# A cross-attention kernel with 8192 keys: the first slots in smaller pieces, the rows of maxima and sums beside V, the last unit's output in one PSUM bank

## The chip, the cores and the metric

The kernel runs on one core of a Trainium2 chip. The core has five engines that this text names: TensorE (PE in the profile; its weight loads are PEld), VectorE (DVE), ScalarE (ACT), GpSimd (POOL) and the queue engine SP, which issues most of the DMAs. Each engine works through its own instructions in order, and engines wait for one another by semaphores. TensorE writes only to PSUM, a small memory of eight banks of 2 KB per partition; everything else lies in SBUF. The metric is device time in microseconds (us) of the whole launch, the median of several runs.

## What is computed

A small transformer layer stack on 2 x 512 latent tokens of 512 features: cross-attention to 2 x 8192 context tokens, then windowed self-attention, then a mixture of experts. Only the first stage is touched. It is

```python
q = layernorm(x) @ Wq.T + bq            # 2 x 512 x 512
k, v = ctx @ Wk.T + bk, ctx @ Wv.T + bv # 2 x 8192 x 512
att = einsum('bhqd,bhkd->bhqk', q, k) / sqrt(32)   # 16 heads
att = where(mask == 0, -inf, att)
out = einsum('bhqk,bhkd->bhqd', softmax(att), v)
x = x + out @ Wo.T + bo
```

All inputs are float32. The mask of these inputs is all ones, but the kernel handles any.

## The kernel before

The heads are worked off four at a time, since four heads of 32 features fill the 128 rows of TensorE. A batch with one such group of heads is a *unit*; there are 8. The keys come in chunks of 512, so a unit has 16 chunks, and there are 128 chunks in all. The softmax is exact and takes two passes over the keys of a unit: the first finds the row maxima, the second computes the exponentials with the maximum taken off, their sums and the weighted values. A unit's keys are projected ahead of the first pass and kept for the second; one load of a context chunk serves the keys of one unit and the values of the unit before it, where both are of one batch.

The main loop (line 399) runs over 128 + 18 *slots*. In slot n the kernel loads context for slot n + 1, projects the keys of chunk n (`project_k`, two halves of 256 keys), finds the maxima of chunk n - 1 (`max_part`, four times, once for each 128 queries), projects the values of chunk n - 16 (`project_v`, two halves), and does scores, exponentials and values of chunk n - 18 (`scores` and `values`, four times). `LAG` is that 18. The body of a slot has four *quarters*, i = 0 to 3, each with one `max_part`, one `scores` and one `values`; keys go with quarters 0 and 1, values with quarters 2 and 3.

So the slots fall into three kinds. In the first slots (1 to 17) there are only keys and maxima. From slot 18 to 127 all of it runs. From slot 128 there are no more keys and maxima.

The steps that matter here:

- *First slots.* `max_part` has its own branch for them. TensorE writes the scores of two heads into a pair buffer of two banks (L276, tile sx), and takes the mask off with four bf16 matmuls from a row of it (L282, operand mk, loaded from mrow_h by L221); VectorE reduces each pair (L287, into mst). There are three pair buffers (`a_pairs`), and the pool for everything else has two banks (`a_ps1`). The queries (L173, 4 matmuls of the whole 128 x 128 array with 512 columns, L177 copies them out) are made one group of heads at a time: the first ahead of the loop, the others out of the list `later`, one entry at the end of each slot. The list also holds the layernorm and the four transposes (L98) of the second batch.
- *Keys and values.* Both use TensorE in column tiles: a matmul with 32 weight columns fills a quarter of the array, and four run side by side (L239 for keys, tile pk; L255 for values, tile pv). ScalarE copies keys out (L243), VectorE values with their bias (L260, tile vt).
- *Maxima from slot 18 on.* Scores in one bank for each head (L295), and one VectorE operation with the mask, which also takes the maximum (L300).
- *End of the first pass of a unit* (`max_finish`, at the end of the slot after its last chunk, so at slots 16, 32, ...): VectorE reduces mst (L309), splits the float32 maximum into three bf16 parts (L311, L313, tile mrep), TensorE turns them into rows (L316, tile pm), ScalarE copies them to SBUF (L321, tile mT). `scores` takes them off with bf16 matmuls (L337).
- *Second pass.* TensorE scores (L331, tile sc), ScalarE the exponential (L344, tile pt; acc for the first of a unit), TensorE the values (L353, tile av), VectorE adds them to the unit's output (L361, tile avs). GpSimd adds the exponentials into acc (L365); near the end of the loop VectorE does that.
- *End of a unit* (`finish`, in the slot of the next unit's second chunk, so at slots 35, 51, ...): TensorE sums acc over the keys (L373, tile sm), ScalarE copies (L377, tile rl), VectorE takes reciprocals (L379), GpSimd multiplies (L381).

The order on each engine is the order of the program, except that a scheduler at build time moves an instruction ahead of ones that can't start yet. A pool of PSUM banks gives a bank out again as soon as its last reader is done, and TensorE waits for that. From slot 18 on one pool has all 8 banks, and a quarter takes 9 or 10 of them in turn.

Ahead of the loop SP loads in this order: x of the first batch, wq, wk, the first context chunk, x of the second batch, wv. The first mask load follows the second context chunk. The mask rows in DRAM (mrow, mrow_h) are written by `mask_rows` after the first query.

After the loop eight output projections (L106, tile po) follow; the last unit's `finish` stands after the second of them.

## Time and profile before

| | |
|---|---|
| median of 3 runs | 3814.18 us (3814.16 to 3819.29) |
| the profiled execution's own time | 3813.35 us |
| its span, first to last instruction | 3811.6 us |
| first slots, 24.0 to 254.2 us of the span | 230.2 us |
| slots 18 to 127, to 2438.8 | 2184.6 us |
| last slots, to the first output projection at 2666.1 | 227.3 us |
| the rest of the program | 1145.5 us |
| mean granted TensorE clock | 0.995 |
| bytes moved | 438.07 MB, mean 115 GB/s |

A row of the timeline has the start, the duration of a merged group, engine, line, operation, output and inputs, shapes, how many instructions, and in brackets how long the engine had stood idle and for whom. Durations of merged groups overlap on TensorE, so the cost of a block is the distance to the start of the next one. "DVE 60%" is a mean over stages of different kinds: by the windows, VectorE is busy 163.75 of the first slots' 230.20 us and 208.90 of the last slots' 227.30.

### The profile page before, as it was taken

To read this page: it belongs to the slowest core of one execution; us is meant where nothing else is said; L and a number is where in the kernel's file an instruction comes from. 1 tells how busy PE (TensorE), PEld (TensorE's weight loads), DVE (VectorE), ACT (ScalarE), POOL (GpSimd) and SP (SyncE) were. 2 spreads that over 40 slices of the span, in tenths; PEclk is the share of its full clock that TensorE was granted. 3 is DMA by queue.
4 is the path that set the end of the run, shared out by engine and by line. 5 is a ranking of instruction groups with operands and counts; after the bars stand their busy time and mean duration, and the time that the engine had idled before them with its cause. 6 is when DMAs were issued, how large, how long until landed. Compare 5 with 4: busy or idle time off the path is not lost.

```text
span 3811.6 us, 99469 instructions
## 1 busy us (share of the span) xinstructions
PE 3741.4 (98%) x43060; PEld 1835.4 (48%) x43060; DVE 2293.9 (60%) x5420; ACT 1601.8 (42%) x2965; POOL 2069.0 (54%) x523
## 2 busy tenths in 40 slices
PE   8999999999999999999999999999999999999998
PEld 3345554554554555555455455444454444444444
DVE  5777777777777777777777777799853600000000
ACT  1125555555555555555555555677463001111110
POOL 0029998998998998899899899600200000000000
PEclk9999999999999999999999999999999999999999
DMA  5222211222213333222222122222201178888885
GB/s 189 89 73 71 71 62 66 71 71 71 69 63 111 122 120 104 61 68 71 71 71 71 57 71 71 71 79 71 80 25 43 61 240 287 288 286 287 287 284 172
DMA packets 143735, 438.07 MB, mean 115 GB/s; under 512 B 9408, under 2 KB 11728, under 8 KB 117856
## 3 DMA queue, kind: packets, MB, share of 16 engines
q1 hardware_dynamic: 137856, 419.33, 33.0%
q0 software_dynamic: 5200, 12.30, 1.3%
q8 instruction: 337, 5.52, 0.6%
q14 instruction: 102, 0.84, 0.1%
q10 hardware_dynamic: 240, 0.08, 0.0%
HBM read 423.21 MB, written 8.47 MB: 113 GB/s over the span
## 4 chain that ended last, share of the span: by engine, by line
PE 87%; DVE 2%; ACT 2%; issue 1%; DMA 0%; POOLq 0%; DVEq 0%; ACTq 0%
PE av L353 13%; PE sx L295 12%; PE sc L331 12%; PE pv L255 11%; PE pf L857 11%; PE pk L239 10%; PE py L875 5%; PE pf L810 3%; PE sc L337 3%; PE po L106 2%; PE pqkv L535 2%; PE pso L833 1%; PE tp L98 1%; DVE junk L300 1%; ACT sb L611 1%
## 5 line engine op out<-in xcount | busy, mean ns | idle before, releaser
L365 POOL TENSOR_TENSOR acc<-acc,pt 128x2048 f32<-128x2048 f32 x437 | 1991.9, 4558 | 445.6 <-ACT pt L344 444.9
L344 ACT ACTIVATE pt<-sc,mbias 128x512 f32<-128x512 f32 x2016 | 1220.1, 690 | 951.2 <-PE sc L337 949.7
L300 DVE CUSTOM_DVE_ANT_0 junk<-sx,mk 128x512 bf16<-128x512 f32 x1776 | 1228.1, 691 | 550.0 <-PE sx L295 352.7
L331 PE MATMUL sc<-qT,kt 32*128 32x512 f32 x4096 | 546.4, 594 | 0.0
L353 PE MATMUL av<-pt,vt 128*32 128x512 f32 x4032 | 540.6, 605 | 2.8 <-DVE mst L300 2.8
L255 PEld LDWEIGHTS pv<-wv_sb,ctx_t 128*32 128x32 f32 x16384 | 457.6, 110 | 155.0 <-DVE mst L300 101.4
L295 PE MATMUL sx<-kt,qT 32*128 32x512 f32 x3552 | 509.1, 640 | 0.9 <-DVE vt L260 0.9
L239 PE MATMUL pk<-ctx_t,wk_sb 128*32 128x256 f32 x8192 | 497.5, 384 | 2.1 <-DVE mst L300 2.1
L255 PE MATMUL pv<-wv_sb,ctx_t 128*32 128x128 f32 x16384 | 495.1, 273 | 1.3 <-DVE avs L361 1.3
L857 PE MATMUL pf<-wt,xinT 128*128 128x512 f32 x1024 | 459.4, 593 | 1.1
L239 PEld LDWEIGHTS pk<-ctx_t,wk_sb 128*32 128x32 f32 x8192 | 263.3, 111 | 295.7 <-DVE mst L300 104.7
L361 DVE TENSOR_TENSOR avs<-av,avs 128x512 f32<-128x512 f32 x504 | 345.4, 685 | 2.7 <-PE av L353 2.5
L331 PEld LDWEIGHTS sc<-qT,kt 32*128 32x128 f32 x4096 | 245.6, 184 | 201.0 <-issue 160.3
L864 DVE TENSOR_TENSOR eo<-pf,sg 128x512 f32<-128x512 f32 x64 | 44.3, 692 | 459.0 <-PE pf L857 459.0
L857 PEld LDWEIGHTS pf<-wt,xinT 128*128 128x128 f32 x1024 | 193.0, 190 | 221.0 <-issue 213.2
L786 POOL DMA_INDIRECT xin<-h_dram,idx x16 | 15.9, 992 | 435.1 <-PE tp L98 310.0
L881 POOL DMA_INDIRECT out_x<-y,idx x16 | 25.3, 1579 | 408.9 <-DVE y L880 408.9
L353 PEld LDWEIGHTS av<-pt,vt 128*32 128x32 f32 x4032 | 81.7, 108 | 325.9 <-DVE mst L300 281.0
L875 PE MATMUL py<-wt,eoT 128*128 128x512 f32 x512 | 222.3, 592 | 0.0
L862 ACT ACTIVATE sg<-pf 128x512 f32<-128x512 f32 x64 | 38.2, 597 | 426.9 <-PE pf L857 426.9
L337 PE MATMUL sc<-mT,neg 32*128 32x512 bf16 x2048 | 207.8, 374 | 0.0
L295 PEld LDWEIGHTS sx<-kt,qT 32*128 32x128 f32 x3552 | 139.9, 182 | 138.2 <-DVE mst L300 92.3
(159 smaller groups left out, 2471.1 us busy)
## 6 DMA issues: line engine op xcount, KB each, us to landing
ctx_t<-in_ctxT SPq DMA_DIRECT2D x160, 1024.0 KB, 6.0
wt<-in_gw SPq DMA_DIRECT2D x64, 1024.0 KB, 4.9
wt<-in_up SPq DMA_DIRECT2D x64, 1024.0 KB, 4.9
wt<-in_down SPq DMA_DIRECT2D x64, 1024.0 KB, 6.3
mk<-mrow SPq DMA_DIRECT2D x111, 256.0 KB, 3.5
ctx<-in_wqkv SPq DMA_DIRECT2D x3, 1024.0 KB, 5.1
mk<-mrow_h SPq DMA_DIRECT2D x17, 128.0 KB, 2.9
x_sb<-in_x SPq DMA_DIRECT2D x2, 1024.0 KB, 10.7
```

What stands on the lines that cost most here:

```text
L239: nc.tensor.matmul(pk[ts(h, DK), :], lhsT=wk_sb[:, c, ds(g * P + h * DK, DK)], rhs=ctx_t[slot, b][:, c, hs], start=(c == 0), stop=(c == DC ...
L255: nc.tensor.matmul(pv[ts(k, DK), i, :], lhsT=ctx_t[slot, b][:, c, ds((2 * half + i) * P + k * DK, DK)], rhs=wv_sb[:, c, ts(g, P)], start=( ...
L295: nc.tensor.matmul(sm, lhsT=qT[r, g, ds(b * S + c * P, P)], rhs=k_t[s][r, :], start=True, stop=True)
L300: nc.vector.tensor_tensor_reduce(out=junk, in0=ss[h], in1=mk_t[s], scale=1.0, scalar=-3.0e38, op0=ALU.add, op1=ALU.max, accum_out=mst[u][: ...
L331: nc.tensor.matmul(sc, lhsT=k_t[s][r, ts(ch, P)], rhs=qT[r, g, ts(b, S)], start=True, stop=False)
L337: nc.tensor.matmul(ss[h], lhsT=neg[r, :], rhs=m_t[u][r, :], start=False, stop=True)
L344: nc.scalar.activation(pt[:, h, :], ss[h], AF.Exp, bias=mbias[:, b, cc : cc + 1], scale=SCALE)
L353: nc.tensor.matmul(av[ts(h, DK), :], lhsT=v_t[s][:, ch, ts(h, DK)], rhs=pt_t[s, ch][:, h, :], start=True, stop=True,)
L361: nc.vector.tensor_tensor(avs[u], av, avs[u], ALU.add)
L365: eng.tensor_tensor(acc[u], acc[u], pt_t[s, ch], ALU.add)
L857: nc.tensor.matmul(pf, lhsT=xinT[:, c, :], rhs=wt[:, c, :], start=False, stop=(c == DC - 1))
L875: nc.tensor.matmul(py, lhsT=eoT[:, fq * 4 + c, :], rhs=wt[:, c, :], start=False, stop=(fq == FQ - 1 and c == 3),)
```

## The change

- In slots 0 to 15 keys are projected in quarters of 128 keys, one in each quarter of a slot, one slot's first quarter at the end of the slot before. The queries use column tiles too and are cut into eight pieces of 4 matmuls (half of the queries, a quarter of the features); `later` gives out one piece in every quarter. The general pool `a_ps1` has one bank, and a second one, `a_psq`, has one for queries and transposes.
- Loads: wk and the first context chunk come ahead of wq, the mask rows and the first mask load ahead of the query.
- `max_finish` moves one slot later and keeps its reduction on VectorE; the split into three parts goes to GpSimd, from SBUF. The matmuls that make rows of it, in column tiles, go into the free half of the bank that `project_v` uses, by `beside`, two halves; ScalarE copies them from there.
- The sums of a unit go the same way, beside V in the slot of the next unit's second chunk; the reciprocals and the product follow in the slot after.
- From slot 128 `project_v` makes one block of 128 keys in each quarter. From slot 130 one bank is set aside, and the last unit's values accumulate in it by TensorE; VectorE does no additions for that unit, and its product is made on VectorE.

```diff
-        ps = first_ps.enter_context(tc.tile_pool(name="a_ps1", bufs=2, space=PSUM))
+        ps = first_ps.enter_context(tc.tile_pool(name="a_ps1", bufs=1, space=PSUM))
+        ps_q = first_ps.enter_context(tc.tile_pool(name="a_psq", bufs=1, space=PSUM))
...
         def query_in(b, c):
             xn = tmp.tile([P, D], F32, tag="row", name="xn")
             normalized(xn, b * (NT // B) + c, *ln[b])
-            transposed(xnT[b][:, :, ts(c, P)], xn, ps)
-        def query(b, g):
-            pq = ps.tile([P, S], F32, tag="ps", name="pq")
-            for c in range(DC):
+            transposed(xnT[b][:, :, ts(c, P)], xn, ps_q)
+        pq = {}
+        def query(b, g, half, c):
+            if c == 0:
+                pq[0] = ps_q.tile([P, S // 2], F32, tag="ps", name="pq")
+            for h in range(4):
                 nc.tensor.matmul(
-                    pq, lhsT=wq_sb[:, c, ts(g, P)], rhs=xnT[b][:, c, :],
-                    start=(c == 0), stop=(c == DC - 1),
-                )
-            nc.scalar.activation(qT[:, g, ts(b, S)], pq, AF.Identity, bias=bq_c[:, g : g + 1])
+                    pq[0][ts(h, DK), :], lhsT=wq_sb[:, c, ds(g * P + h * DK, DK)],
+                    rhs=xnT[b][:, c, ts(half, S // 2)], start=(c == 0), stop=(c == DC - 1),
+                )
+            if c == DC - 1:
+                nc.scalar.activation(
+                    qT[:, g, ds(b * S + half * (S // 2), S // 2)], pq[0], AF.Identity,
+                    bias=bq_c[:, g : g + 1],
+                )
...
-                tp = ps.tile([P, P], F32, tag="ps", name="tpk")
+                tp = (ps, ps_q)[b].tile([P, P], F32, tag="ps", name="tpk")
...
-        def project_k(slot, half):
+        def project_k(slot, part, parts=2):
             u, j = chunks[slot]
             b, g = units[u]
-            if half == 0:
+            if part == 0:
                 k_t[slot] = kp.tile([P, KC], F32, tag="k", name="kt")
-            hs = ts(half, KC // 2)
-            pk = ps.tile([P, KC // 2], F32, tag="ps", name="pk")
+            hs = ts(part, KC // parts)
+            pk = ps.tile([P, KC // parts], F32, tag="ps", name="pk")
             for c in range(DC):
                 for h in range(4):
                     nc.tensor.matmul(
...
                     )
             nc.scalar.activation(k_t[slot][:, hs], pk, AF.Identity, bias=bk_c[:, g : g + 1])
-        def project_v(slot, half):
+        def project_v(slot, lo, n):
             s = slot - NKC
-            if half == 0:
+            if lo == 0:
                 v_t[s] = vp.tile([P, KC // P, P], F32, tag="v", name="vt")
-            pv = ps.tile([P, 2, P], F32, tag="ps", name="pv")
-            for i in range(2):
+            pv = ps.tile([P, 4, P], F32, tag="ps", name="pv")
+            for i in range(n):
                 for c in range(DC):
                     for k in range(4):
                         nc.tensor.matmul(
                             pv[ts(k, DK), i, :],
-                            lhsT=ctx_t[slot, b][:, c, ds((2 * half + i) * P + k * DK, DK)],
+                            lhsT=ctx_t[slot, b][:, c, ds((lo + i) * P + k * DK, DK)],
                             rhs=wv_sb[:, c, ts(g, P)], start=(c == 0), stop=(c == DC - 1),
                         )
+            if lo >= 2 or n == 2:
+                beside(slot, lo // 2 if n == 2 else lo - 2, pv[:, 2:4].rearrange("p n k -> p (n k)"))
             nc.vector.tensor_tensor(
-                v_t[s][:, ts(half, 2), :], pv,
-                bv_b[:, ts(g, P)].unsqueeze(1).to_broadcast([P, 2, P]), ALU.add,
+                v_t[s][:, ds(lo, n), :], pv[:, 0:n, :],
+                bv_b[:, ts(g, P)].unsqueeze(1).to_broadcast([P, n, P]), ALU.add,
             )
...
                 )
-        def max_finish(u):
-            rest = ps.tile([P, 4, 4], F32, tag="ps", name="mcol")
-            nc.vector.tensor_reduce(rest, mst[u], AX.X, ALU.max)
-            for i in range(3):
-                nc.vector.tensor_copy(mrep[:, :, :, i], rest)
+        def max_finish(u, step):
+            if step == 0:
+                rest[u] = tmp.tile([P, 4, 4], F32, name="mcol")
+                nc.vector.tensor_reduce(rest[u], mst[u], AX.X, ALU.max)
+            for i in ((0,), (1, 2))[step]:
+                nc.gpsimd.tensor_copy(mrep[:, :, :, i], rest[u])
                 if i < 2:
-                    nc.vector.tensor_tensor(rest, rest, mrep[:, :, :, i], ALU.subtract)
-            pm = ps.tile([P, S], F32, tag="ps", name="pm")
-            for c in range(4):
-                nc.tensor.matmul(
-                    pm[:, ts(c, P)], lhsT=mrep[:, c, :, :].rearrange("p h r -> p (h r)"),
-                    rhs=ident_h, start=True, stop=True,
-                )
-            m_t[u] = mp.tile([P, S], BF16, tag="mT", name="mT")
-            nc.scalar.copy(m_t[u], pm)
+                    nc.gpsimd.tensor_tensor(rest[u], rest[u], mrep[:, :, :, i], ALU.subtract)
+        def beside(slot, half, dst):
+            hs = ts(half, S // 2)
+            u = units_at(slot - 2, NKC - 1)
+            if u is not None:
+                if half == 0:
+                    m_t[u] = mp.tile([P, S], BF16, tag="mT", name="mT")
+                for c in range(2):
+                    for h in range(4):
+                        nc.tensor.matmul(
+                            dst[ts(h, DK), ts(c, P)], lhsT=mrep[:, 2 * half + c, h, :],
+                            rhs=ident_h, start=True, stop=True,
+                        )
+                nc.scalar.copy(m_t[u][:, hs], dst)
+            u = units_at(slot - LAG - NKC, 1)
+            if u is not None:
+                if half == 0:
+                    rl[u] = tmp.tile([P, S], F32, tag="row", name="rl")
+                for h in range(4):
+                    nc.tensor.matmul(
+                        dst[ts(h, DK), :], lhsT=ones32, rhs=acc[u][:, h, hs],
+                        start=True, stop=True,
+                    )
+                nc.scalar.copy(rl[u][:, hs], dst)
+        def units_at(s, j):
+            return s // NKC if 0 <= s < NS and s % NKC == j else None
...
         def values(s, ch):
             u, j = chunks[s]
             first = j == 0 and ch == 0
-            av = ps.tile([P, S], F32, tag="ps", name="av")
+            last = u == len(units) - 1
+            av = avs[u] if last else ps.tile([P, S], F32, tag="ps", name="av")
             for h in range(4):
                 nc.tensor.matmul(
                     av[ts(h, DK), :], lhsT=v_t[s][:, ch, ts(h, DK)], rhs=pt_t[s, ch][:, h, :],
-                    start=True, stop=True,
-                )
-            if first:
+                    start=first or not last, stop=not last or (j == NKC - 1 and ch == 3),
+                )
+            if last:
+                pass
+            elif first:
                 avs[u] = mp.tile([P, S], F32, tag="avs", name="avs")
                 nc.vector.tensor_copy(avs[u], av)
             else:
...
                 eng = nc.gpsimd if s + LAG <= NS else nc.vector
                 eng.tensor_tensor(acc[u], acc[u], pt_t[s, ch], ALU.add)
-        def finish(u, step):
+        def finish(u, i):
             b, g = units[u]
-            if step == 0:
-                sm = ps.tile([P, S], F32, tag="ps", name="sm")
-                for h in range(4):
-                    nc.tensor.matmul(
-                        sm[ts(h, DK), :], lhsT=ones32, rhs=acc[u][:, h, :], start=True, stop=True
-                    )
-                rl[u] = tmp.tile([P, S], F32, tag="row", name="rl")
-                nc.scalar.copy(rl[u], sm)
-            for i in {0: (), 1: (0, 1), 2: (2, 3), 3: ()}[step]:
-                nc.vector.reciprocal(rl[u][:, ts(i, P)], rl[u][:, ts(i, P)])
-            if step == 3:
-                nc.gpsimd.tensor_tensor(qT[:, g, ts(b, S)], avs[u], rl[u], ALU.mult)
+            nc.vector.reciprocal(rl[u][:, ts(i, P)], rl[u][:, ts(i, P)])
+            if i == 3:
+                eng = nc.vector if u == len(units) - 1 else nc.gpsimd
+                eng.tensor_tensor(qT[:, g, ts(b, S)], avs[u], rl[u], ALU.mult)
+        def finish_last():
+            u = len(units) - 1
+            sm = ps.tile([P, S], F32, tag="ps", name="sm")
+            for h in range(4):
+                nc.tensor.matmul(
+                    sm[ts(h, DK), :], lhsT=ones32, rhs=acc[u][:, h, :], start=True, stop=True
+                )
+            rl[u] = tmp.tile([P, S], F32, tag="row", name="rl")
+            nc.scalar.copy(rl[u], sm)
+            for i in range(4):
+                finish(u, i)
         load(0)
+        wq_sb = load_w(wq, pp, "p")
         load_x(1)
         wv_sb = load_w(wv, cp, "wv_sb")
+        mask_rows()
+        load_mask(0)
         query_norm(0)
         for c in range(NT // B):
             query_in(0, c)
-        query(0, 0)
-        mask_rows()
-        load_mask(0)
-        later = [lambda g=g: query(0, g) for g in range(1, G)]
+        for i in range(4):
+            project_k(0, i, 4)
+        halves = [(half, c) for half in range(2) for c in range(DC)]
+        for half, c in halves:
+            query(0, 0, half, c)
+        later = [lambda g=g, p=p: query(0, g, *p) for g in range(1, G) for p in halves]
         later += [lambda: query_norm(1)]
         later += [lambda c=c: query_in(1, c) for c in range(NT // B)]
-        later += [lambda g=g: query(1, g) for g in range(G)]
+        later += [lambda g=g, p=p: query(1, g, *p) for g in range(G) for p in halves]
         waiting = None
         for slot in range(NS + LAG):
             if slot == LAG:
                 first_ps.close()
-                ps = es.enter_context(tc.tile_pool(name="a_ps", bufs=8, space=PSUM))
+                steady_ps = ExitStack()
+                ps = ps_q = steady_ps.enter_context(tc.tile_pool(name="a_ps", bufs=8, space=PSUM))
+            if slot == NS + LAG - NKC:
+                steady_ps.close()
+                ps = es.enter_context(tc.tile_pool(name="a_ps3", bufs=7, space=PSUM))
+                last_ps = es.enter_context(tc.tile_pool(name="a_last", bufs=1, space=PSUM))
+                avs[len(units) - 1] = last_ps.tile([P, S], F32, name="avl")
             if slot + 1 < NS + NKC:
...
-                if s >= NKC and chunks[s][1] == 1:
-                    finish(chunks[s][0] - 1, i)
-                if i < 2 and slot < NS:
+                u = units_at(s - NKC, 2)
+                if u is not None:
+                    finish(u, i)
+                if slot < NKC:
+                    if i < 3 and slot > 0:
+                        project_k(slot, i + 1, 4)
+                    elif i == 3 and slot + 1 < NKC:
+                        project_k(slot + 1, 0, 4)
+                elif i < 2 and slot < NS:
                     project_k(slot, i)
-                if i == 3 and slot > 0 and later:
+                if later:
                     later.pop(0)()
-                if i >= 2 and NKC <= slot < NS + NKC:
-                    project_v(slot, i - 2)
-            if 1 <= slot <= NS and chunks[slot - 1][1] == NKC - 1:
-                max_finish(chunks[slot - 1][0])
+                if i >= 2 and NKC <= slot < NS:
+                    project_v(slot, 2 * i - 4, 2)
+                elif NS <= slot < NS + NKC:
+                    project_v(slot, i, 1)
+                u = units_at(slot - 2, NKC - 1)
+                if u is not None and i < 2:
+                    max_finish(u, i)
             if n == 1:
-                for i in range(4):
-                    finish(len(units) - 1, i)
+                finish_last()
```

More of the change, by code (lines that the diff above doesn't have):

```diff
@@ L152, in perceiver_kernel @@
         junk = cp.tile([P, KC], BF16, name="junk")
-        wq_sb = load_w(wq, pp, "p")
         wk_sb = load_w(wk, cp, "wk_sb")
@@ L201, in perceiver_kernel @@
         ctx_t, mk_t, k_t, v_t = {}, {}, {}, {}
-        mst, m_t, acc, pt_t, avs, rl = {}, {}, {}, {}, {}, {}
+        mst, m_t, acc, pt_t, avs, rl, rest = {}, {}, {}, {}, {}, {}, {}
         def load(slot):
```

## The prediction

> **What bounds the kernel now.** I read the page first, its busy rows and its slices.
>
> ```profile
> PE 3741.4 (98%) x43060; PEld 1835.4 (48%) x43060; DVE 2293.9 (60%) x5420; ACT 1601.8 (42%) x2965; POOL 2069.0 (54%) x523
> PE   8999999999999999999999999999999999999998
> ```
>
> TensorE looks full everywhere, but a matmul's end is modelled, so a full digit can still hold waiting. What counts is the distance from one block's start to the next, and that I took from the timeline, first in the steady slots (18 to 127), where nothing waits:
>
> ```profile
> 284.09 1.14 PE L295 MATMUL sx<-kt,qT 32*128 32x512 f32 x8
> 285.06 1.04 PE L331 MATMUL sc<-qT,kt 32*128 32x512 f32 x8
> 285.91 0.39 PE L337 MATMUL sc<-mT,neg 32*128 32x512 bf16 x4
> 286.24 1.07 PE L353 MATMUL av<-pt,vt 128*32 128x512 f32 x8
> 287.12 1.93 PE L255 MATMUL pv<-wv_sb,ctx_t 128*32 128x128 f32 x64
> ```
>
> Starts differ by 0.97, 0.85, 0.33, 0.88 and, to the next sx at 288.98, 1.86. These are my TensorE prices: 4.89 us a quarter slot (4.87 with pk), 19.51 a slot; VectorE is busy 14.45 of it by the windows. 97 of the 109 slots 19 to 127 last 19.5 to 19.6 us and are TensorE's own work, which the change leaves alone. What it can win is elsewhere, in three places.
>
> First slots (1 to 17, 24.0 to 254.2 by the first sx of L276 and of L295):
>
> ```profile
> 49.72 0.40 PE L282 MATMUL sx<-mk,neg 1*128 1x512 bf16 x4
> 50.14 4.83 DVE L287 TENSOR_REDUCE mst<-sx 128x2 f32<-128x1024 f32 x4 [0.80 <-PE sx L282]
> 51.42 0.70 PE L276 MATMUL sx<-kt,qT 32*128 32x512 f32 x2 [0.46 <-DVE mst L287]
> 52.70 3.70 PE L173 MATMUL pq<-xnT,p 128*128 128x512 f32 x8
> 56.33 1.14 PE L276 MATMUL sx<-kt,qT 32*128 32x512 f32 x8
> 57.71 2.36 DVE L287 TENSOR_REDUCE mst<-sx 128x2 f32<-128x1024 f32 x2 [2.74 <-PE sx L282]
> ```
>
> Quarters 2 and 3 have no projection between them, so TensorE waits for VectorE's maxima; then the query (3.63 us) holds the maxima back and VectorE stands 2.74 us. Each waits for the other in turn: 13.88 us for a slot.
>
> Unit ends, at slots 32 + 16k and 35 + 16k:
>
> ```profile
> 547.22 0.43 DVE L309 TENSOR_REDUCE mcol<-mst 128x16 f32<-128x256 f32 x1
> 549.39 0.40 PE L316 MATMUL pm<-ident_h,mrep 128*128 128x128 bf16 x4 [1.71 <-DVE mrep L311]
> 549.72 1.14 PE L295 MATMUL sx<-kt,qT 32*128 32x512 f32 x8
> 591.87 1.04 PE L373 MATMUL sm<-acc,ones 128*32 128x512 f32 x8
> 594.07 2.58 DVE L379 RECIPROCAL rl<-rl 128x128 f32<-128x128 f32 x3 [0.23 <-ACT rl L377]
> 597.25 1.06 PE L353 MATMUL av<-pt,vt 128*32 128x512 f32 x8 [0.47 <-DVE mst L300]
> ```
>
> Slot 32 takes 21.7 us: 2.1 over, 1.71 of it TensorE waiting for VectorE's split, the rest the pm matmuls. Slot 35 takes 21.47, 1.96 over: the sums (0.86) and 1.10 of stalls behind the reciprocals, which come before the maxima that free PSUM. Six units end so inside the steady part.
>
> Last slots (128 to 145):
>
> ```profile
> 2600.73 1.14 PE L331 MATMUL sc<-qT,kt 32*128 32x512 f32 x8
> 2602.89 1.93 PE L255 MATMUL pv<-wv_sb,ctx_t 128*32 128x128 f32 x64
> 2603.81 0.68 DVE L361 TENSOR_TENSOR avs<-av,avs 128x512 f32<-128x512 f32 x1
> 2604.76 1.14 PE L331 MATMUL sc<-qT,kt 32*128 32x512 f32 x8
> ```
>
> A slot takes 12.92 here. TensorE's blocks make 4 x 2.17 + 2 x 1.86 = 12.4. VectorE has 4 x 2.28 (acc) + 4 x 0.68 (avs) + 2 x 0.42 (vt) = 12.7, in front-loaded quarters, which costs TensorE the 0.5.
>
> **The change, part by part.** *First slots.* A quarter becomes sx 0.97 + neg 0.33 + a quarter of keys + a query piece. A quarter of keys is 32 instructions of 128 columns, the form of pv: 1.86 / 2 = 0.93. A query piece is 8 instructions of 256 columns, a quarter of a pk half: 0.47. Sum 2.69. VectorE's two reductions of 1.21 make 2.42, so TensorE is the bound, and three pair buffers are just enough: a buffer is wanted again 2.7 us after its block began and is reduced by 2.6. Slots 1 to 15: 52 query quarters x 2.69 = 139.9; four with transposes (0.86) at 3.08 = 12.3; five without a piece, about 9.9 in all. That is 162. Slots 16 and 17 (1.29 x 4 + 4 x 1.86) 12.6 and, with the maxima's rows, 13.1. Together 187.7 against 230.2: minus 42.5. This includes the half clock: the granted-clock events show five stretches at 0.5 in these slots, 20.5 us long, about 10 us lost; the page's clock for the part is 0.96.
>
> Here a rule of the Trainium skill speaks against the change. "TensorEngine Tiling (Array Packing)", section Instruction Overhead, warns of about 60 cycles for each matmul and advises not to split what is already small; the query goes from 8 instructions of the whole array to 64 of 32 columns. Charged in full (an estimate, 25 ns by the 2.4 GHz in the table that opens "TensorE: Matmul & The Clock Gate"), 56 more instructions x 7 queries would be 9.8 us. The row of pk says otherwise: 32 such instructions in 1.86 us, 58 ns each for 256 columns, so a query is 3.72 against 3.63. I take the row: 0.7 us in all, already in the sum.
>
> *Start.* wk and ctx go ahead of wq; the mask rows ahead of the query. SP reaches the first mask load before the second ctx, and must wait there for mrow_h; behind it in SP's queue stands every ctx load. The mask (6.9 us to land after 3.6) allows mbias at 11 instead of 12.1, the rows are written by about 17.5, the six megabytes ahead occupy the queues until about 20.8, so ctx comes at about 24 as before. TensorE now waits for ctx (about 13.1, from the DMA bytes in order) before the transposes that began at 10.5. From there: keys 3.7, transposes 3.4, query 3.7, four pieces 1.9, a quarter of keys 0.9: 13.6, plus 1.5 for single banks (four hand-overs, 0.3 to 0.5 each by the ACT copies) and 2 for the cold clock. First maxima at about 30 instead of 24.0; the mask wait of 2.70 is then gone (counted in the 230.2). Plus 6, bounds 3 to 8.
>
> *Maxima.* The wait of 1.71 and pm's 0.33 go from slot 32 (minus 2.1). The split goes to GpSimd as five operations of 128x16. No row has that shape; between the two sizes of POOL's TENSOR_TENSOR (4558 ns at 2048, 1304 at 512) the fixed part is about 0.22 us, so 1.3 us in all, at most 6.5 if each cost as much as the 512 one. In the order of the built program they stand behind acc 58 of the unit and wait for VectorE's reduction; GpSimd, at 18.23 of 19.51, falls behind by about 3 us and gains 0.3 a quarter. Queued behind are acc's adds; they free pt, which is wanted some 12 us later, and TensorE reads mrep two quarters later: hidden. Without this cover it is the old 1.7 again. TensorE now runs 16 matmuls of 32 weight columns: pm's 83 ns each would be 1.3 us, pv's pitch of 29 ns 0.5; the form is pv's, I take 0.5 to 0.6.
>
> *Sums.* 8 matmuls (16 instructions) of 256 columns behind V: 0.93 instead of 0.86. The reciprocals are not spread as the source says: the built order has two around the end of each V half. VectorE has 3.4 us extra over three quarters with 0.4 to 0.8 free each; I leave 0.45 of the 1.10.
>
> "PSUM — Partial Sum Buffer", section PSUM bank collisions, forbids two engines in one bank and quadrant at once, even to read; here ScalarE copies the rows while VectorE wants V from the same bank. The built order makes vt wait for ScalarE's copy, so the rule shows as a wait: about 0.5 us (a copy of 256 columns is 0.3 to 0.5). Queued behind vt are the next maxima, but the trace gives VectorE 0.60 idle just there: I take nothing, 0.5 if the cover fails, two halves for 15 rows, 30 times: 15 us at worst.
>
> A unit's end: minus 2.1 + 0.55, minus 1.96 + 0.93 + 0.45, together minus 2.1; six of them minus 12.7 (bounds 5 and 17).
>
> *Last slots.* The last unit's outputs accumulate in one bank: 64 avs additions of 0.68 leave VectorE. A quarter is then TensorE 2.17 + 0.93 = 3.10, ScalarE 4 exponentials 2.42, VectorE 2.28 + 0.28 = 2.56. Slot 128 (19.08, VectorE behind) to about 16.1: minus 3; slots 131 and 132 (29.7, sums and reciprocals) to 26.2: minus 3.5; eleven slots by 0.5: minus 5.4; slots 130, 144 and 145: minus 1.3. Seven banks and the change of pools give back about 1. Minus 12.2. Late next is TensorE. The final division, now on VectorE, is ready before the fifth po, as now.
>
> *Sum.* -42.5 + 6 - 12.7 - 12.2 = -61.4. Span 3811.6 becomes 3750.2; the profiled run's own time lies 1.75 over its span, so 3752; the median of the runs shown is 0.8 above the profiled run, so 3752.8.
>
> **The rivals.** *The first slots stay a ping-pong:* the third pair buffer is 0.1 us too tight, or cold clock stays. A quarter of 2.95 costs 60 x 0.26 = 16: 3769. For it: the 0.46 waits for mst; against it: 2.42 under 2.69. *Unit ends keep their price:* GpSimd or the vt wait takes over, and nothing of the 12.7 comes: 3765.5. *Everything hides:* start at 26, no reciprocal stall: 3744. *Slower:* the single key and query banks. Each block must wait for ScalarE's copy of the last; that is 0.5 of copy against 1.7 us of other blocks. Only if a copy came so late that a quarter lasted over 2.69 + 61.4 / 60 = 3.71 would the kernel lose; at 4.0 it stands at about 3831. ScalarE is busy 23.87 of the 230.20 us, which speaks against it. *Nothing done:* the scheduler could keep the old order; the built order shows quarters and pieces alternating, so this is excluded.
>
> **How the numbers follow.** A measurement of this kernel can tell about 0.2%, 7.6 us. Forecast 0.58 (3744 to 3763), ping-pong 0.16, unit ends 0.13, all hidden 0.09, slower 0.04. The range 3740 to 3773 takes in the first four with their unknowns (start -3 to +2, pm 0.8 a unit, vt up to 15). Faster by over 0.2% 0.94, within 0.02, slower 0.04.
>
> **What would show it.** Slots 2 to 5 of 10.7 us; no 0.5 clock after the first maxima; first maxima near 30; slot 32 at 19.5 and slot 33 at about 20; slots 35 and 36 about 1.4 over; slots 133 to 143 at 12.4. Wrong if the first slots last over 12 us, TensorE waits for POOL at mrep, or VectorE's idle before vt grows a following sx wait.

## The result and the profile after

The changed kernel takes 3777.05 us in the median, the kernel before 3815.3 in the runs beside it: a ratio of 0.990, with an interval of 0.988 to 0.992. It is faster by 38 us, 1.0%; the prediction had 61 and a range that ends at 3773. One of the changed kernel's four executions took 9710.65 us, in a slow state of which nothing more is known; ratio and interval leave it out, and the median of the other three is 3776.6. The profiled execution took 3775.76 us; its span is 3774.0 (before 3811.6), a gain of 37.6.

By the starts of slots, 31.6 of these come ahead of slot 18, 6.0 between slot 18 and slot 128, and nothing from slot 128 to the end. (From slot 18 on a slot begins here with its first sc. The table ahead puts the border at 2438.8, where the last quarter of slot 128 begins, and so counts most of that slot to the slots before it: 2184.6 there, 2171.5 here.)

| part | before | after | change | predicted |
|---|---|---|---|---|
| until the first maxima | 24.0 | 32.15 | +8.2 | +6 |
| slots 1 to 17 | 230.2 | 190.4 | -39.8 | -42.5 |
| slots 18 to 127 (by the first sc) | 2171.5 | 2165.5 | -6.0 | -12.7 |
| slot 128 to the end | 1384.9 | 1384.9 | 0 | -12.2 |

The last row hides two things. From slot 128 to the first output projection the changed kernel takes 240.9 us where the kernel before takes 239.4; what follows is 1.4 shorter, which is no more than this part differs between the runs (1143.9 to 1145.4). So the last slots became 1.4 us longer.

The page's busy rows say little, since PE is full in both:

```profile
PE 3720.3 (99%) x44684; PEld 1854.2 (49%) x44684; DVE 2250.9 (60%) x5349; ACT 1614.9 (43%) x3020; POOL 2076.8 (55%) x562
```

*First slots.* The timeline of slot 2, one quarter of it and the start of the next:

```profile
45.81 1.14 PE L288 MATMUL sx<-kt,qT 32*128 32x512 f32 x8
46.77 0.40 PE L294 MATMUL sx<-mk,neg 1*128 1x512 bf16 x4
47.10 1.08 PE L248 MATMUL pk<-ctx_t,wk_sb 128*32 128x128 f32 x32
47.19 2.36 DVE L299 TENSOR_REDUCE mst<-sx 128x2 f32<-128x1024 f32 x2 [0.37 <-PE sx L294]
47.99 0.61 PE L178 MATMUL pq<-xnT,p 128*32 128x256 f32 x8
48.54 1.14 PE L288 MATMUL sx<-kt,qT 32*128 32x512 f32 x8
```

TensorE no longer stands: by the starts, 0.96, 0.33, 0.89 and 0.55 add up to a quarter of 2.73, and VectorE waits 0.37 a quarter instead of 0.80 and 2.74 in turn. The windows give the whole stretch and two others that came out otherwise than predicted (us; then busy time and count for PE, PEld, DVE, ACT, POOL; granted clock, DMA share, GB/s): the first slots, slot 129 and slots 133 to 143.

```profile
32.20:222.60 190.40, 189.31 (x3540) 101.84 (x3536) 163.17 (x143) 33.29 (x84) 1.22 (x5) 1.00 0.34 106
2405.00:2426.60 21.60, 15.71 (x231) 7.37 (x228) 13.67 (x15) 10.88 (x19) 7.38 (x7) 0.92 0.25 75
2468.00:2607.60 139.60, 139.60 (x2292) 67.50 (x2288) 109.64 (x88) 106.33 (x177) 0.00 (x0) 1.00 0.27 85
```

The clock of the first slots is 1.00 now, against 0.96. What the first slots cost before depends on that clock: in the profile of x6 below, whose program is the old one there, they hold 37.5 us of half clock and last 235.1 us, against 20.5 and 230.2. Slot 129, which took 12.97 us before, takes 21.55, with 15.71 of TensorE's work in it and a clock of 0.92.

*Slot 129.* Its timeline, from quarter 0 to the start of slot 130:

```profile
2406.72 0.26 POOL L324 CAST mrep<-mcol 128x16 bf16<-128x16 f32 x1
...
2408.14 4.53 POOL L403 TENSOR_TENSOR acc<-acc,pt 128x2048 f32<-128x2048 f32 x1
...
2412.71 2.29 DVE L403 TENSOR_TENSOR acc<-acc,pt 128x2048 f32<-128x2048 f32 x1 [4.54 <-POOL acc L403]
2414.92 0.28 DVE L272 TENSOR_TENSOR vt<-pv,bv_b 128x128 f32<-128x128 f32 x1
2415.12 0.68 DVE L399 TENSOR_TENSOR avs<-av,avs 128x512 f32<-128x512 f32 x1
2415.26 0.71 PE L365 MATMUL sc<-qT,kt 32*128 32x512 f32 x3 [2.79 <-DVE vt L272]
...
2426.24 0.28 DVE L272 TENSOR_TENSOR vt<-pv,bv_b 128x128 f32<-128x128 f32 x1
2426.58 2.09 PE L365 MATMUL sc<-qT,kt 32*128 32x512 f32 x8 [3.10 <-DVE vt L272]
```

And the same place in the kernel before, three rows of it, where slot 129 starts at 2445.78:

```profile
2435.20 13.81 POOL L365 TENSOR_TENSOR acc<-acc,pt 128x2048 f32<-128x2048 f32 x3
2445.78 1.14 PE L331 MATMUL sc<-qT,kt 32*128 32x512 f32 x8
2449.74 2.29 DVE L365 TENSOR_TENSOR acc<-acc,pt 128x2048 f32<-128x2048 f32 x1 [0.85 <-ACT pt L344]
```

Read the first of them backwards from 2415.26. TensorE stands 2.79 us for a bank that V's copy (vt) frees. The copy is short, but it is queued on VectorE behind its first addition into acc, and that waits 4.54 us for GpSimd's last addition into the same acc. Before, GpSimd was through at 2449.01, and VectorE waited for ScalarE alone. GpSimd is late because slot 128 got shorter (19.08 to 15.94 us) while its four additions need 18.2, and the split of the maxima (1.42 us) stands ahead of the last. TensorE stands again, 3.10 us, at the first scores of slot 130, which are the first in the new banks. The clock events give 0.5 from 2416.3 to 2419.7, right behind the first stall, and from 2426.6 to 2430.0, right behind the second, so the quarters behind the waits are longer too.

*A unit's end.* The sums and reciprocals of slot 35, from the timeline:

```profile
569.35 0.61 PE L347 MATMUL pv<-acc,ones 128*32 128x256 f32 x8
570.03 0.37 ACT L351 COPY rl<-pv 128x256 f32<-128x256 f32 x1 [0.74 <-PE pv L347]
570.44 0.42 DVE L272 TENSOR_TENSOR vt<-pv,bv_b 128x256 f32<-128x256 f32 x1 [0.87 <-ACT rl L351]
570.78 0.94 DVE L408 RECIPROCAL rl<-rl 128x128 f32<-128x128 f32 x1
571.64 0.63 DVE L312 CUSTOM_DVE_ANT_0 junk<-sx,mk 128x512 bf16<-128x512 f32 x1
572.19 0.95 DVE L408 RECIPROCAL rl<-rl 128x128 f32<-128x128 f32 x1
573.75 1.96 PE L265 MATMUL pv<-wv_sb,ctx_t 128*32 128x128 f32 x64 [0.35 <-DVE mst L312]
```

VectorE first waits 0.87 us for ScalarE, which reads the rows out of the bank that V shares, and then does two reciprocals around one maximum. TensorE waits behind that. Slots 32 to 37 take 0.00, 0.40, 0.12, 1.71, 0.85 and 0.10 us more than 19.51, together 3.2; before it was 2.2 in slot 32, 0.1 in slot 34 and 1.96 in slot 35, together 4.3. The other five unit ends gain 0.6 to 1.0 us, all six 5.4. Slot 18, at 19.45 for 20.16, gives another 0.7, and with a few slots of 0.1 either way these are the 6.0 of the table.

### The profile page after: what moved, and what is told of

Read it like the earlier page. It is cut to its first block, busy times and chain, and to the rows that moved or that the text cites. A ratio compares the mean times of both kernels' runs of the same rounds, so it can differ in the third digit from the quotient of the medians.

```text
span 3774.0 us, 102663 instructions
## 1 busy us (share of the span) xinstructions
PE 3720.3 (99%) x44684; PEld 1854.2 (49%) x44684; DVE 2250.9 (60%) x5349; ACT 1614.9 (43%) x3020; POOL 2076.8 (55%) x562
## 4 chain that ended last, share of the span: by engine, by line
PE 94%; DVE 2%; ACT 2%; issue 1%; POOL 1%; DMA 0%; POOLq 0%; SPq 0%; ACTq 0%; DVEq 0%
PE sx L307 12%; PE pk L248 12%; PE sc L365 12%; PE pv L265 12%; PE av L389 11%; PE pf L919 11%; PE py L937 5%; PE pf L872 3%; PE sc L371 3%; PE sx L288 2%; PE avl L389 2%; PE pqkv L597 2%; PE pso L895 1%; PE po L106 1%; PE tp L98 1%
## 5 line engine op out<-in xcount | busy, mean ns | idle before, releaser
L248 PE MATMUL pk<-ctx_t,wk_sb 128*32 128x256 f32 (+1 forms) x9216 | 499.7, 357 | 5.4 <-DMA ctx_t<-in_ctxT 3.1
L389 PE MATMUL av<-pt,vt 128*32 128x512 f32 x3528 | 471.2, 606 | 0.9
L248 PEld LDWEIGHTS pk<-ctx_t,wk_sb 128*32 128x32 f32 x9216 | 284.3, 110 | 298.2 <-DVE mst L312 103.7
L399 DVE TENSOR_TENSOR avs<-av,avs 128x512 f32<-128x512 f32 x441 | 302.5, 686 | 6.6 <-PE av L389 6.6
L252 ACT ACTIVATE kt<-pk,bk_c 128x256 f32<-128x256 f32 (+1 forms) x288 | 129.5, 450 | 224.1 <-PE pk L248 224.0
L389 PEld LDWEIGHTS av<-pt,vt 128*32 128x32 f32 x3528 | 69.5, 108 | 283.5 <-DVE mst L312 277.6
```

Source lines behind the costliest of these rows:

```text
L248: nc.tensor.matmul(pk[ts(h, DK), :], lhsT=wk_sb[:, c, ds(g * P + h * DK, DK)], rhs=ctx_t[slot, b][:, c, hs], start=(c == 0), stop=(c == DC ...
L389: nc.tensor.matmul(av[ts(h, DK), :], lhsT=v_t[s][:, ch, ts(h, DK)], rhs=pt_t[s, ch][:, h, :], start=first or not last, stop=not last or (j ...
L399: nc.vector.tensor_tensor(avs[u], av, avs[u], ALU.add)
```

## The experiments

In what follows "after" is the changed kernel (3777.05 us, span 3774.0). The runs are in three groups, beside which the kernel before took 3816.23 (x1 to x4), 3818.43 (x5 to x8) and 3814.39 us (x9 to x11), so totals of different groups are comparable to some 4 us only. The argument rests on the lengths of slots in the profiles. The theory: the missing 23.8 us are lost in three places, (a) at the hand-over of acc from GpSimd to VectorE in slot 129, with what hangs on it, (b) at the unit ends, on VectorE, and (c) in the start. The rivals: the early change of banks costs the last slots, and the change in the first slots hands work on to later ones.

**x1: VectorE takes over at a unit's border.**

```diff
-                eng = nc.gpsimd if s + LAG <= NS else nc.vector
+                eng = nc.gpsimd if u < len(units) - 1 else nc.vector
```

> All else as in the changed kernel; VectorE takes over the additions of exponentials at the last unit's first chunk (slot 130) instead of one chunk earlier, so that no unit's acc passes from GpSimd to VectorE. My theory: the two long quarters of slot 129 (8.8 and 6.4 us) come from VectorE's first addition, which waits 4.5 us for GpSimd's last one with V's copies queued behind it. Then slot 129 falls from 21.5 to 13 to 14 us and the kernel from 3777 to 3768 to 3770 us. Rival (the seven-bank pool or the rows of maxima are what costs there): slot 129 stays at 20 us or more, 3775 to 3778.

Measured: 3773.03 us (span 3771.6). Slots 129 and 130 shrink to 14.07 and 13.03 us, as the theory had it, but slot 131 goes from 13.54 to 20.06, so the kernel misses both numbers, that of the theory and that of the rival. The two engines now add into different tiles, so neither waits by a semaphore. The timeline of the three engines in slots 130 and 131:

```profile
2416.94 15.70 POOL L403 TENSOR_TENSOR acc<-acc,pt 128x2048 f32<-128x2048 f32 x3
...
2428.17 0.28 DVE L272 TENSOR_TENSOR vt<-pv,bv_b 128x128 f32<-128x128 f32 x1
2428.92 5.87 DVE L403 TENSOR_TENSOR acc<-acc,pt 128x2048 f32<-128x2048 f32 x1 [0.47 <-ACT pt L378]
2434.72 0.28 DVE L272 TENSOR_TENSOR vt<-pv,bv_b 128x128 f32<-128x128 f32 x1
2434.92 2.27 DVE L403 TENSOR_TENSOR acc<-acc,pt 128x2048 f32<-128x2048 f32 x1
...
2435.05 1.23 PE L365 MATMUL sc<-qT,kt 32*128 32x512 f32 x3 [2.27 <-DVE vt L272]
```

VectorE's addition takes 5.87 us instead of 2.29, until 2.15 us after GpSimd's last one has ended (2432.64): it got next to nothing done meanwhile. GpSimd's last addition, which began 0.45 us after one of VectorE's, took 6.46 instead of 4.55. From 2425.73, where the first of these three additions begins, to the end of the 5.87 it is 9.06 us, for 2.29 + 4.55 + 2.29 = 9.13 of work: the additions exclude each other. So the wait only changed its kind, and V's copy behind it is late as before.

**x2: no bank set aside, no change of banks at slot 130;** VectorE adds up the last unit's output as in the kernel before.

```diff
-            if slot == NS + LAG - NKC:
-                steady_ps.close()
-                ps = es.enter_context(tc.tile_pool(name="a_ps3", bufs=7, space=PSUM))
-                last_ps = es.enter_context(tc.tile_pool(name="a_last", bufs=1, space=PSUM))
-                avs[len(units) - 1] = last_ps.tile([P, S], F32, name="avl")
...
-            last = u == len(units) - 1
+            last = False
```

> The changed kernel without the reserved bank: the pool keeps eight banks to the end and VectorE adds the last unit's outputs as before. My theory: slot 129 stays at 21 to 22 us, since its stall is there before the pools change; slot 130's first quarter loses its 1.6 us of excess; slots 133 to 143 go from 12.69 to about 13.0 us, as VectorE's quarter is then 2.28 + 0.68 + 0.28 = 3.24 us. Together 3777 to 3781. Rival (the pool change causes the stall): slot 129 and 130 fall by 8 us or more together and the kernel is at 3770 to 3773.

Measured: 3774.59 us, between the two. Slot 129 keeps its third quarter of 8.88 us, which is the hand-over, but its last one falls from 6.43 to 3.27 and slot 130 from 14.29 to 12.68, and the second stretch of half clock is gone. So both are true: the hand-over costs about 5.6 us, and the change of banks some 4.8 with the half clock behind it. Slots 131 and 132 give 1.95 back, where VectorE now has its additions to the output beside the reciprocals, and slot 145 gives back 0.5. Slots 133 to 143, which were to become 13.0 without the bank, stay at 12.70 for 12.69: VectorE is busy 135.87 of their 139.70 us with the additions back, and TensorE all of it. So the bank wins nothing there; what shortened these slots from 12.92 is V in quarters.

**x6: the last slots alone,** put on the kernel before: V in quarters from slot 128 and the bank set aside; the split and the rows stay where they were.

```diff
-                if i >= 2 and NKC <= slot < NS + NKC:
-                    project_v(slot, i - 2)
+                if i >= 2 and NKC <= slot < NS:
+                    project_v(slot, 2 * i - 4, 2)
+                elif NS <= slot < NS + NKC:
+                    project_v(slot, i, 1)
...
+            if slot == NS + LAG - NKC:
...
+                avs[len(units) - 1] = last_ps.tile([P, S], F32, name="avl")
```

> The kernel before with only V's quarters and the reserved bank from slot 128/130 on; the maxima's split and the rows stay on their old engines and banks. If slot 129's loss in the changed kernel comes from a shortened slot 128 (15.9 us, less than GpSimd's four additions of 18.2) and the split queued ahead of them, this kernel, whose slot 128 keeps the split and the old row banks (about 19 us), has slot 129 near 13 to 15 and gains about 4 to 6 us from the end: 3809 to 3812. Rival: the reserved bank or V's blocks of one quarter cost it themselves: slot 129 over 17, and 3815 or more.

Measured: 3816.16 us against 3818.43 beside it, ratio 1.000 (0.999 to 1.001): no change. Slot 128 lasts 18.56 us here, and the third quarter of slot 129 is 3.16: no hand-over wait, as the theory says. But slot 129 still takes 17.63 us, with 4.79 in its first quarter, behind the old split on VectorE, and 6.52 in the quarter ahead of the change of banks; slot 130 takes 14.32, and its first scores wait here too:

```profile
2469.80 1.93 PE L331 MATMUL sc<-qT,kt 32*128 32x512 f32 x8 [3.18 <-DVE vt L260]
```

That is the rival's number, so the bank change is a cause of its own.

**x7: a second sum.** VectorE sums the four tiles of slot 129 by themselves; the matmuls with ones take both.

```diff
-            if not first:
+            if s + LAG == NS + 1:
+                if ch == 0:
+                    acc["own"] = pt_t[s, ch]
+                else:
+                    nc.vector.tensor_tensor(acc["own"], acc["own"], pt_t[s, ch], ALU.add)
+            elif not first:
```

> After, with the four probability tiles of slot 129 (the last chunk of the last unit but one) summed into a tile of their own by VectorE (three additions, none waits for GpSimd) and both tiles summed by the matmuls with ones (eight more). Theory: VectorE's wait for GpSimd's last addition (4.5 us) goes, V's copies behind it come in time, PE stays busy and the half clock does not come: slot 129 at 12.7 to 14, slot 130 at 13, kernel 3767 to 3770. Rival, a loss by the early change of banks or by V's blocks in quarters: slot 129 stays over 18 and the kernel within 2 us of after.

Measured: 3770.54 us, just outside the theory's 3767 to 3770; slot 129 takes 16.35 us, which is neither number. The third quarter of slot 129 goes from 8.81 to 3.27; the last one is 6.78, and slot 130 14.32. The timeline at the border of slots 129 and 130:

```profile
2411.80 2.72 DVE L406 TENSOR_TENSOR pt<-pt 128x2048 f32<-128x2048 f32 x1 [0.82 <-ACT pt L380]
...
2418.49 2.29 DVE L406 TENSOR_TENSOR pt<-pt 128x2048 f32<-128x2048 f32 x1 [0.17 <-ACT pt L380]
2420.70 0.28 DVE L272 TENSOR_TENSOR vt<-pv,bv_b 128x128 f32<-128x128 f32 x1
...
2421.04 1.38 PE L367 MATMUL sc<-qT,kt 32*128 32x512 f32 x8 [2.93 <-DVE vt L272]
```

There is no wait for GpSimd any more (VectorE's first addition, 2.72 us, only meets the last 0.57 of GpSimd's). What remains is slot 130's scores, the first in new banks: they wait 2.93 us for the V copy of slot 129, which stands behind an addition of 2.29.

**x9: x7 and x2 together.**

> The second sum of x7 and, with it, no change of banks at slot 130 and no bank kept for the last unit's output (VectorE adds it up, as before). Theory: after x7 the rest of slot 129's loss (16.35 us, last quarter 6.78) and slot 130's (14.32) is the wait of slot 130's scores, in newly opened banks, for the last V copy out of the old ones, behind an addition of 2.3 us; without the change of banks slot 129 and 130 are at 12.7 to 13 each, with no half clock; slots 131 and 132 lose about 2 as in the kernel without the kept bank: 3766.5 to 3768.5. Rival: the V copies are late by VectorE's additions alone, whatever the banks: slot 129 stays over 15 and the kernel at 3769 to 3771.

Measured: 3768.38 us (3767.86 to 3768.96), at the upper end of what the theory gave. Slots 129 and 130 take 13.35 and 12.68 us, and there is no half clock near them. The windows of slots 129 and 130:

```profile
2405.40:2418.80 13.40, 13.40 (x232) 6.73 (x228) 9.16 (x12) 10.12 (x18) 7.40 (x7) 1.00 0.24 79
2418.80:2431.40 12.60, 12.60 (x212) 6.14 (x208) 9.81 (x12) 9.72 (x18) 0.00 (x0) 1.00 0.27 86
```

TensorE is busy all of it. The two causes are taken away, and 9.8 us of slots 129 and 130 with them; 1.9 comes back in slots 131 and 132, and 0.5 in slot 145.

**x4: one reciprocal a quarter,** each held behind the last maximum of its own quarter.

```diff
+            held[0] = nc.cur_bb.bb.instructions[-1]
...
-            nc.vector.reciprocal(rl[u][:, ts(i, P)], rl[u][:, ts(i, P)])
+                with tc.issue_after(held[0]):
+                    nc.vector.reciprocal(rl[u][:, ts(i, P)], rl[u][:, ts(i, P)])
```

> The changed kernel with each of the four reciprocals of a unit (all but the last two units) held, in VectorE's order, behind the maxima of its own quarter, one in each quarter of slot 36, as the source has it, instead of two on either side of one maximum. If the burst is what stalls TensorE, slots 35 and 36 fall from 41.6 us together to 40.2 to 40.6 (39.0 and the 1.07 of the sums, and a little), five times, and the kernel by 5 to 7 us to about 3771. If the wait of V's copy for ScalarE does it, they stay above 41 us.

Measured: 3771.45 us; slots 35 and 36 take 40.59 us instead of 41.58, in all six units, and the steady part is 5.5 shorter. The theory's numbers hold, though V's copy still waits 0.87 us for ScalarE in slot 35. Slot 129, whose program is that of after, takes 22.91 us in this profile instead of 21.55: its first stall comes with 6.8 us of half clock instead of 3.4. So what a stall there costs is known to some 1.4 us only.

**x3: the rows in a bank of their own.**

```diff
-                beside(slot, lo // 2 if n == 2 else lo - 2, pv[:, 2:4].rearrange("p n k -> p (n k)"))
+                if (units_at(slot - 2, NKC - 1) is not None
+                        or units_at(slot - LAG - NKC, 1) is not None):
+                    own = ps.tile([P, S // 2], F32, tag="ps", name="own")
+                    beside(slot, lo // 2 if n == 2 else lo - 2, own)
```

> The changed kernel with the rows of maxima and of sums in a PSUM bank of their own instead of the free half of V's. VectorE's copy of V then need not wait for ScalarE's copy of the rows. If that wait (0.6 to 0.9 us, twice at each unit's sums) is what makes slots 35 and 36 long, they fall from 41.6 us together to about 40.6, and the kernel by about 6 us to 3771. If the burst of reciprocals does it, they stay within 0.3 us and the kernel within 3775 to 3778; an eleventh bank in a ring of eight could also cost up to 0.3 us for each row.

Measured: 3773.85 us, between the two numbers. Slots 35 and 36 take 40.92 us, and 33 and 34 0.24 less than after. V's copy has no wait left, and the reciprocals now wait for ScalarE instead:

```profile
571.74 0.42 DVE L275 TENSOR_TENSOR vt<-pv,bv_b 128x256 f32<-128x256 f32 x1
572.57 0.95 DVE L411 RECIPROCAL rl<-rl 128x128 f32<-128x128 f32 x1 [0.41 <-ACT rl L354]
```

Slots 17 and 18, with a bank more in use, lose 2.5 us (15.76 and 20.17 for 14.00 and 19.45).

**x5: the first slots alone,** on the kernel before (the rest as before).

```diff
-        def project_k(slot, half):
+        def project_k(slot, part, parts=2):
...
-        def query(b, g):
+        def query(b, g, half, c):
...
-                if i == 3 and slot > 0 and later:
+                if later:
```

> The kernel before with only the changed start and first slots (keys in quarters, query pieces in every quarter, the new order of loads); rows, maxima's split and last slots as before. If the gain of the whole change comes from the first slots, as the two traces say (slot 18 starts 31.6 us earlier, nothing after it differs here): 3815.3 - 31.6, so 3783 to 3786, with first maxima near 32 us and slot 18 near 223 us, and no gain or loss from slot 18 on. Rival: the first slots only push work behind slot 18 (value copies, bank order), which gives part of it back: over 3790.

Measured: 3783.97 us, ratio to before 0.991 (0.990 to 0.993). First maxima come at 31.7 us, and from slot 18 on every slot has the length that it has in the kernel before. At slot 18 it is 29.4 us ahead of the kernel before, and it stays so: the gain of the first slots is kept whole; nothing is handed on. The 2.2 that after has more are those of slot 17 (14.00 us for 16.62), where the old `max_finish` stands.

**x8: no query piece in slot 0.**

```diff
-                if later:
+                if later and slot > 0:
```

> After, with no piece of the next query projection in slot 0 (four pieces of eight matmuls, which now stand ahead of the first maxima on TensorE and wait for the one bank). Theory: they are on the path to the first maxima, 4 x 0.47 us and a wait of 0.6: first maxima at 29.5 to 30 instead of 32.15, and the pieces end one slot later, in slots bound by other work: 3774.5 to 3775. Rival: the first maxima wait for loads or ScalarE in any case, or the pieces cost the same later: 3776.5 to 3778.

Measured: 3774.46 us, first maxima at 29.53 instead of 32.15. The timelines ahead of them, of after:

```profile
27.32 1.93 PE L178 MATMUL pq<-xnT,p 128*32 128x256 f32 x32 [0.57 <-ACT qT L183]
29.07 0.62 PE L248 MATMUL pk<-ctx_t,wk_sb 128*32 128x128 f32 x16
29.85 1.50 PE L178 MATMUL pq<-xnT,p 128*32 128x256 f32 x24 [0.16 <-ACT qT L183]
31.17 0.62 PE L248 MATMUL pk<-ctx_t,wk_sb 128*32 128x128 f32 x16
31.61 0.61 PE L178 MATMUL pq<-xnT,p 128*32 128x256 f32 x8
32.15 1.13 PE L288 MATMUL sx<-kt,qT 32*128 32x512 f32 x7
```

and of x8:

```profile
26.67 1.93 PE L178 MATMUL pq<-xnT,p 128*32 128x256 f32 x32 [0.57 <-ACT qT L183]
28.42 1.18 PE L248 MATMUL pk<-ctx_t,wk_sb 128*32 128x128 f32 x32
29.53 1.14 PE L288 MATMUL sx<-kt,qT 32*128 32x512 f32 x8
```

The four pieces (24 + 8 instructions) stand on the path. Of the 2.6 us, about 1.4 is left at slot 16, since the pieces come back in slot 15 (10.05 for 9.09 us) and a little in slot 1.

**x10: x9, x4 and x8 together,** and **x11: with x3's bank as well.**

> x9 with one reciprocal a quarter behind its own quarter's maxima (as in x4) and no piece of a query projection in slot 0 (as in x8). The parts stand in different slots, so their gains should add: x4's 5.6 and x8's 2.5 from x9's 3767.5, so 3758.5 to 3761. Rival: x4's gain was partly the shift of the clock's windows and not the reciprocals: 3762 to 3765.

> x10 with the rows of maxima and sums in a bank of their own (as in x3), so that V's copy need not wait for ScalarE's copy of the rows. Alone it took 0.93 us from each unit's slots 33 to 36 and gave 2.5 back in slots 17 and 18. If the two waits (the reciprocals, the shared bank) add up: 0.6 to 0.9 x 6 more, less 2.5: 3756 to 3760. Rival: with the reciprocals apart the copy of the rows hides, and only the 2.5 is left: 3761 to 3763.

Measured: 3762.42 us for x10 and 3761.34 for x11 (3761.02 to 3761.57; ratio to before 0.986, interval 0.984 to 0.988). By its total x10 lies at the rival's number, by its slots it does not: 35 and 36 take 40.58 us as in x4, and at slot 128 it is 7.3 us ahead of x9, 5.5 of them from the unit ends as in x4 alone and 1.8 from the start. The program from the first output projection on, which is the same in both, lasts 1145.2 us in this profile and 1144.1 in that of x9; that is 1.1 of what the sum misses. x11 takes 0.5 a unit more and loses 2.5 in slots 17 and 18, which is its rival's number: the two waits do not add up. It is the fastest of all that ran, 15.7 us under after by the medians, which are of different groups.

## Why the prediction was wrong

The sign was right, and so was the largest term, the first slots, with its mechanism. The other sums were off.

**Last slots, -12.2 against 0 (+1.4 up to the first output projection): the main miss.** The step that failed is the one that cost slot 128 at "minus 3" and slot 129 at nothing, and named TensorE as what is late next. It looked at VectorE's queue, which the change relieves, and not at GpSimd's, which it doesn't. Slot 128 did get 3.1 shorter; GpSimd's four additions and the split, 19.6 us of work, did not. Before, GpSimd ended 3.2 us into slot 129, ahead of VectorE's first addition; after, it ended 7.6 us into it. Slot 129 gave back 8.6 and slot 130 1.3. "Seven banks and the change of pools give back about 1" was the second failing term: it is about 4.8 with the half clock (x2), and x6 shows it without the hand-over. x7 and x9 remove the two one after the other. How much of GpSimd's delay is the split (1.42 us by the trace) and how much the shorter slot was not tried apart. The price was not in a rival either: "GpSimd takes over" was weighed at the unit ends only, where a slot of 19.5 us covers 18.2.

The third term is "eleven slots by 0.5": slots 133 to 143 take 12.69 and not 12.4, which is 2.4 us of the 5.4. Nor do they owe it to the "64 avs additions" that leave VectorE: with them back, in x2, these slots are as short. A block of one quarter of V is 0.99 by the starts, not half of 1.86, and a quarter 3.16 instead of 3.10. (A quarter of keys, followed by more column tiles, is 0.89; where row tiles follow it, as in the first quarter of slot 6, it is 1.01. So some 0.1 us seems to fall on each change from column to row tiles, which V in quarters makes four times a slot and not twice.) Slots 131 and 132 gained 2.6 of 3.5.

**Unit ends, -12.7 against -5.4** (the table's -6.0 has 0.7 of slot 18). The split and pm went as said: slot 32 at 19.51, minus 2.2; slots 33 and 34 at 0.52 over, where 0.55 stood (0.94 in one of the six units); the five operations on GpSimd took 0.23 to 0.26 us each, where 1.3 in all was estimated. The failing step is the sums: "I leave 0.45 of the 1.10", and for the wait of V's copy "I take nothing". Slots 35 and 36 have 2.56 over, where 0.93 + 0.45 stood; 1.2 a unit, six times, is the miss. x4 takes 1.0 of it away by the reciprocals' order alone, x3 0.7 by the bank alone, and both together, in x11, take 1.2 and leave 1.40. That this is the predicted 1.38 is chance, for the prediction had the reciprocals in their burst and the rows in V's bank. The Trainium skill's rule that no two engines may be in one bank and quadrant at once, reads included ("PSUM — Partial Sum Buffer", section PSUM bank collisions raise a hardware error), was rightly read as a wait, of 0.5 us, since the built order keeps the two apart (no run here lets them collide); 0.87 and 0.62 were measured. But the 0.60 of idle time that was to cover it was VectorE's own wait for sx, in a slot without a reciprocal behind V's copy. Here two of them, 0.94 us each, stand behind that copy and ahead of the next maxima, and TensorE waits (0.35 at 573.75). This is read from the trace; x3 and x4 show what each of the two is worth.

**Start and first slots, +2.2 and +2.7.** The first context chunk let TensorE begin at 14.76 us instead of 13.1; the 17.4 from there to the first maxima compare with 17.1 in the sum. Slots 1 to 15 took 162.6 against 162, which is partly luck: a quarter with a piece took 2.73 for 2.69, 2.1 us over the 52 of them, but the sum counted 61 quarters (52 + 4 + 5) where 15 slots have 60, and so had about 2 us too many. The rest is slots 16 and 17: 27.9 against 25.7. On many small matmuls the row was nearer than the rule: keys and a query piece take 1.44 us together, where 1.40 stood; over 56 pieces that is 2.2 us on top of the 0.7, 2.9 in all. Charged by the piece alone, 8 x 0.55 for 3.63, it is 5.4; the estimate by the rule had 9.8.

The rivals: the ping-pong did not stay (VectorE waits 0.37 a quarter, TensorE not at all), and the single banks did not slow it. The unit ends kept more than half of their price, and the wait of V's copy, which that rival named, is a part of it. That all hides was wrong (its terms, 4 us of the start and 0.45 a unit, would also make 3746 and not 3744). The likeliest case was right in the first slots alone, and the loss at slot 129 was in no case.

The 2.2 of slots 16 and 17 were not tried by themselves, but the trace shows where they are. The first quarter of slot 16 takes 4.39 us and the next three 3.15 to 3.17: the quarters ahead of it, at the end of slot 15, have no query piece and in the last no keys (2.65 and 1.41 us), so TensorE has run up to VectorE's maxima and its next scores go at their pace. And the first maxima of slot 18, in newly opened banks, wait 0.93 us for V's copy, as at slot 130. The two make 2.2.

## What to carry to other kernels

When a stage gets shorter, list every engine's work in it, also of engines that were never on the path: the one whose work does not shrink is late at the next hand-over, and the short instruction that is queued behind that wait passes it on to TensorE. Idle time in front of an instruction is cover only as long as what ends it stays where it is. Two causes can stand one behind the other in one slot; take them away together as well as singly, or each looks half right.

## What the hardware showed that was not expected

VectorE's and GpSimd's additions of two SBUF operands ran one after the other, not side by side: 5.87 us for 2.29 and 6.46 for 4.55 in x1, and 2.72 for 2.29 in x7, where they met for 0.57. The Trainium skill says so ("SBUF — State Buffer", section SBUF: two separate sides: the pair of ports that the two engines share is an exclusive lock, taken by a VectorE operation with two SBUF inputs against a GpSimd one that reads SBUF, and the loser blocks for the whole instruction), and the traces agree: another tile does not keep the two engines apart. What VectorE does with one operand in PSUM kept its time beside GpSimd's additions: in after, at 2405.35 and 2405.95, avs took 0.68 and vt 0.28 us while GpSimd's addition ran to 2406.78.

A single stall of TensorE in the midst of full work can bring half clock. From slot 18 to the output projections, every stall of 2.2 us or more (2.22 to 3.19, thirteen of them, in after, x1 to x4 and x6 to x8) was accompanied by 3.4 or 6.8 us of half clock, which begins between 0.6 us before the stall's end and 1.4 us after it. None of the stalls of up to 1.71 us was: there are seven of 1.70 or 1.71 in the kernel before, seven in x5 and six in x6. In x9 to x11, where the longest is 0.93, there is no half clock in this part. In these runs a stall of over 2 us is thus paid for twice, once as waiting and once in the work behind it.
